# Moving small operations and a normalization to GpSimd, and reordering logits and diffusions, in the second top-p attention of a graph network

## The chip, the cores and the metric

The kernel runs on one core of a Trainium2 chip. The metric is the device time of one execution in microseconds; the figure for the kernel is the median of three runs. One further execution was recorded by the profiler. Engines are called PE (matrix products), DVE (VectorE), ACT (ScalarE), POOL (GpSimd) and SP (which issues DMAs).

## The reference

Four graph layers follow each other, each with a residual and a layer normalization, on x of 3327 x 256 and a dense adjacency matrix of 3327 x 3327, all in float32: a mean aggregation, a Mamba block, an attention over the edges, and a diffusion with top-p attention. The change concerns the last:

```
def _top_p_attention(X, W1, W2, W3):
    q = X @ W1.T @ W2.T
    k = X @ W3.T
    probs = softmax(q @ k.T)
    # sorted by size, an entry is kept while the sum of those before it is under 0.9
    A = probs * mask
    return A / maximum(A.sum(-1, keepdims=True), 1e-12)

R = (S + I) / row sums
Xf = Xa = X;  Z = 0
for n in range(2):
    A = _top_p_attention(Xa, W1, W2, W3)
    Xf = R @ Xf
    Xa = A @ Xa
    Z = Z + Xf @ U1[n].T + Xa @ U2[n].T
h = X + Z
out = (h - mean(h)) / sqrt(var(h) + 1e-5) * ln_g + ln_b
# and the layer's residual: x = layernorm(x + out)
```

## The kernel before

Rows are padded to 3328 and handled as 26 tiles of 128 rows. A tile's scores are one buffer `e` of 128 x 3328 in SBUF; each half of it has 1664 columns. The last layer has two attentions, p = 0 and p = 1, each with its own loop over the tiles. The change is in the loop of the second. In it Xf of the first step has already been multiplied by U1 (the array `Y`, stored in `F`), Xa by U2 (`G`), and what both give the result of the first step, plus the residual, lies in DRAM as `sd`, so that for a tile the second attention computes

- `diffused`: R @ Y for 128 rows, 26 products on PE whose left sides `at` come by DMA, 5 blocks at a time (`aggregated`); POOL prepares t = Y * rdeg (L823) and adds s, loaded from sd (L827); DVE writes xf (L832). `xfs` collects these tiles ahead of their use, `DL` says how far.
- `scores`: the logits, four pairs of products of 416 columns on PE (L797) into one PSUM buffer `sc`, which ACT copies to e (L782 through a helper that pins the order).
- `search_long`: finds the value v at which the kept sum passes 0.9 of the total, without sorting. ACT makes a first exponential with half the exponent for a guess (L926), then e itself with its total (L928). A threshold c1 is guessed from the two sums (L932 to L934); ACT counts and sums what lies above c1 (L940, L942); a chain of operations of 128 x 1 on DVE gives a better threshold c2 (L944 to L960); ACT counts again (L973, L975); a second chain gives c3 (L977 to L986). DVE then writes z, the entries below c3, for each half (L992), takes the 8 largest of each segment of 128 (MAX8, L858), ranks them (`ranked`, L869 and L871), runs a prefix sum over the 48 largest (`crossing`, L878 to L881), and so finds v. Ties at v are counted (L1004 to L1014), surplus ones removed by MATCH_REPLACE (L1017), and everything below v is set to zero with the kept sum as by-product (L1025).
- `attended`: A @ G: 26 transposes of e on PE (L842), copies `wt` on ACT, 26 products (L846).
- `second`: h = acc * f + xf on DVE (L1069), its statistics (`stats`, bn_stats L84 and bn_aggr L85), the inverse deviation rs by a power on POOL (L593, L594), h = (h - mean) * g (L1077), h = h * rs + xb (L1078) on DVE, where POOL has made xb = X + b (L1071); then a second normalization, with nb = -mean * rs on POOL (L1085) and the write of the result by ACT (L1086) and a DMA.

The loop is a software pipeline written by hand. In turn i, tile i is searched, tile i - 1 is attended, tile i + 2's logits are made, a tile is diffused and tile i - 2's result written. All of these are Python generators, and each `next` emits one step; `slot` emits some products of the diffusion, a step of `attended` and a step of a search. The order on each engine comes from a scheduler that works on this program; `keep_in_program_order` (also called `here`) fixes an operation's place among those so marked, `high_priority` lets operations go ahead of others that are ready, and `issue_after` ties the MATCH_REPLACE to the step that gives c2. The loop begins at i = -2.

Of the kernel before, what the change touches and what calls it, by code (L numbers as in the profile page):

```python
# [9 lines left out]
F32 = mybir.dt.float32  # L10
# [8 lines left out]
P = 128  # L19
# [18 lines left out]
J3 = 5  # L38
DL = 2
KC = 416  # L40
# [3 lines left out]
def gnn_kernel(ctx: ExitStack, tc: tile.TileContext, n: int, a: dict, out: bass.AP):  # L44
# [36 lines left out]

    def stats(mv, y):
        st = small.tile([P, 6], F32, name="bnst")
        nc.vector.bn_stats(st, y)  # L84
        nc.vector.bn_aggr(mv, st)  # L85
# [498 lines left out]
    with tc.tile_pool(name="l3", bufs=1) as pool, tc.tile_pool(name="l3d", bufs=1, space=DRAM) as dram:  # L584
# [178 lines left out]
        u1, u2 = (load(pool, x) for x in ("U1", "U2"))  # L763
        g3, b3 = (load_row(pool, x) for x in ("ln3_g", "ln3_b"))
        ones = pool.tile([P, 8 * max(RP0, RPT)], F32, name="ones")
        nc.vector.memset(ones, 1.0)
# [12 lines left out]
        tots, vs, kepts = ([pool.tile([P, nt], F32, name=f"{x}{p}") for p in range(2)] for x in ("tot", "v", "kept"))  # L779

        def in_order(op):
            return lambda *x, **k: tc.keep_in_program_order(op(*x, **k))  # L782

        def scores(work, psum, p, q, e):

            copy = in_order(nc.scalar.copy) if p else nc.scalar.copy
            if npad > n:
                nc.gpsimd.memset(e[:, n:], NEG)
            halves = e.rearrange("p (h c) -> p h c", h=2)
            for c0 in range(0, half, KC):  # L790
                pl = psum.tile([P, 2, 512], F32, name="sc", bufs=1)
                ws = [min(KC, n - c0 - h * half) for h in range(2)]

                with tc.high_priority():
                    for h, w in enumerate(ws):
                        k = slice(h * DA, (h + 1) * DA)
                        nc.tensor.matmul(pl[:, h, :w], q[k, :], kT[p][k, c0:c0 + w], start=True, stop=True)  # L797
# [75 lines left out]

        def crossing(work, v, top, base, lim):

            k = top.shape[1]
            cs = work.tile([P, k], F32, name="cs", bufs=1)
            nc.vector.tensor_tensor_scan(cs, ones[:, :k], top, initial=base, op0=ALU.mult, op1=ALU.add)  # L878
            over = work.tile([P, k], F32, name="over", bufs=1)
            nc.vector.scalar_tensor_tensor(over, cs, lim, top, op0=ALU.is_ge, op1=ALU.mult)  # L880
            nc.vector.reduce_max(v, over, axis=AX.X)  # L881
            return cs
# [22 lines left out]

        here = tc.keep_in_program_order
        junks = [None]
        bound = [None]

        def search_long(work, sm, e, total, v, kept, halves=False):  # L910
# [7 lines left out]

            m8, neg, hneg, root = t1(sm, "m8", 8), t("neg"), t("hneg"), t("root")
            nc.vector.max(m8, e[:, :KC])  # L920
            nc.vector.tensor_scalar_mul(hneg, m8[:, 0:1], -0.5)
            nc.vector.tensor_scalar_mul(neg, m8[:, 0:1], -1.0)

            junk = junks[0] = junks[0] or work.tile([P, npad], BF16, name="junk", bufs=1)
            yield
            here(nc.scalar.activation(junk, e, AF.Exp, bias=hneg, scale=0.5, accum_out=root))  # L926
            yield
            here(nc.scalar.activation(e, e, AF.Exp, bias=neg, accum_out=total))  # L928
            yield
            lim = limit(sm, total)  # L930
            c1 = t("c1")
# [15 lines left out]
            nc.vector.reciprocal(rc, c1)  # L947
            nc.vector.tensor_scalar(na, m1, lim, rc, op0=ALU.subtract, op1=ALU.mult)

# [12 lines left out]
            big = t("big")  # L962
            nc.vector.tensor_sub(big, k1, na)
            nc.vector.tensor_scalar(big, big, 32.0, HUGE, op0=ALU.is_lt, op1=ALU.mult)

            s, dm, lo, hi = t("s"), t("dm"), t("lo"), t("hi")
            nc.vector.tensor_sub(s, c2, c1)
            nc.vector.scalar_tensor_tensor(s, s, 0.0, s, op0=ALU.is_equal, op1=ALU.add)
            nc.vector.reciprocal(s, s)
            nc.vector.tensor_scalar(lo, k1, 0.3, 1.0, op0=ALU.mult, op1=ALU.max)  # L970
            nc.vector.tensor_scalar(hi, k1, 1.5, 1.0, op0=ALU.mult, op1=ALU.max)
            yield
# [4 lines left out]
            nc.vector.tensor_scalar(k2, sg, -0.5, npad / 2, op0=ALU.mult, op1=ALU.add)  # L977
            nc.vector.scalar_tensor_tensor(m2, k2, c2, f2, op0=ALU.mult, op1=ALU.add)
            nc.vector.tensor_sub(dm, m1, m2)
            nc.vector.tensor_mul(s, s, dm)  # L980
            nc.vector.tensor_scalar(s, s, lo, hi, op0=ALU.max, op1=ALU.min)
            nc.vector.reciprocal(s, s)
            c3 = t("c3")
            nc.vector.scalar_tensor_tensor(c3, c2, UNDER, m2, op0=ALU.mult, op1=ALU.add)
            nc.vector.tensor_scalar(c3, c3, lim, s, op0=ALU.subtract, op1=ALU.mult)
            nc.vector.scalar_tensor_tensor(c3, c3, c2, big, op0=ALU.add, op1=ALU.max)  # L986
            rest, base = t("rest"), t("base")
            cand = candidates(work)
            for h, r in enumerate((rest, base)):
                part = e[:, h * half:(h + 1) * half]  # L990
                z = work.tile([P, half], F32, name="z", bufs=1)
                nc.vector.scalar_tensor_tensor(z, part, c3, part, op0=ALU.is_lt, op1=ALU.mult, accum_out=r)  # L992
                yield
                segment_tops(cand[:, h * half // SEG * 8:], z, half // SEG)
                yield
            nc.vector.tensor_scalar(base, base, rest, total, op0=ALU.add, op1=ALU.subtract)
            nc.vector.scalar_tensor_tensor(base, big, 1.0, base, op0=ALU.is_lt, op1=ALU.mult)
            nc.vector.tensor_scalar_mul(base, base, -1.0)
            top = ranked(work, cand, RPT)
            cs = crossing(work, v, top, base, lim)  # L1000
            yield

            r, up = t("r"), t("up")
            nc.vector.tensor_sub(cs, cs, top)  # L1004
            nc.vector.tensor_scalar(top, top, v, None, op0=ALU.is_equal)
            nc.vector.scalar_tensor_tensor(cs, cs, lim, top, op0=ALU.is_ge, op1=ALU.mult, accum_out=r)
            upper = cand[:, half // SEG * 8:]
            nc.vector.tensor_scalar(upper, upper, v, 0.0, op0=ALU.is_equal, op1=ALU.add, accum_out=up)
            nc.vector.tensor_sub(up, r, up)
            sums = t1(sm, "sums", 2)  # L1010
            for i, (r, c) in enumerate(((up, 0), (r, half))):
                drop = t1(sm, "drop", 8)
                nc.vector.tensor_scalar(drop, count, r, -HUGE, op0=ALU.is_ge, op1=ALU.mult)  # L1013
                nc.vector.tensor_scalar_add(drop, drop, v)  # L1014
                part = e[:, c:c + half]
# [50 lines left out]
        def second(work, psum, it, acc, f, xf):  # L1066
# [9 lines left out]
            yield  # L1076
            nc.vector.scalar_tensor_tensor(h, h, mv[:, 0:1], g3, op0=ALU.subtract, op1=ALU.mult)  # L1077
            nc.vector.scalar_tensor_tensor(h, h, rs, xb, op0=ALU.mult, op1=ALU.add)  # L1078
            mv = small.tile([P, 2], F32, name="mv")
            stats(mv, h)  # L1080
            rs = small.tile([P, 1], F32, name="rs")
# [37 lines left out]
        with tc.tile_pool(name="l3w", bufs=2) as work, tc.tile_pool(name="l3s", bufs=4) as sm, \  # L1119
# [41 lines left out]
            with tc.tile_pool(name="l3q", bufs=3, space=PSUM) as psum:  # L1161
                es, searches, xfs = {}, {}, []
                result = iter(())
                for i in range(-2, nt + 1):
# [7 lines left out]
                    if i + 2 < nt:  # L1172
                        logits = start(1, i + 2, es, searches, search_long)
                    more = range(len(xfs), min(nt, max(i, 0) + DL + 1))
                    if more:
                        spread = diffused(work, atp, psum, 1, more[0], xfs, 1)

                    def slot(products, looks, pair=False):


                        if pair:
                            next(logits, None)
                        for _ in range(products):
                            next(spread, None)
                        next(values, None)
                        search(looks)
# [7 lines left out]
                    next(logits, None)  # L1194
                    next(result, None)
                    search(i + 2)
                    for _ in range(3):
                        next(spread, None)
                    next(values, None)
                    search(i)  # L1200
                    for _ in result:
                        pass
                    slot(3, i + 1, True)
                    slot(3, i + 1, True)
                    both(logits)
# [157 lines left out]
```

## Time and profile before

| | before |
|---|---|
| median of 3 runs | 3810.78 us (3806.26 to 3815.26) |
| the profiled execution | 3813.28 us, of it the span 3811.5 us |
| first attention | 1994 to 2911 us, PE busy over 99% |
| second attention | 2911 to 3811 us |
| busy: PE, DVE, ACT, POOL | 3482.6, 2626.2, 1739.7, 497.9 us |
| granted clock of PE, mean | 0.961 |

Busy times are sums over the span and differ much by stage. A row of the timeline has the start in the span, the duration, the engine, the line of the kernel, the operation and its output and inputs, then shapes; in brackets the idle time before it and what ended it. A row of the waits has who waited for whom, the sum in microseconds, how often, and the longest.

### The profile page before, as it was taken

What the parts mean: (1) busy time and instruction counts of PE and PEld (TensorE: products, weight loads), DVE (VectorE), ACT (ScalarE), POOL (GpSimd) and SP (SyncE); (2) the same over time, 40 slices, a digit from 0 to 9 for tenths busy, and PEclk for the clock granted to TensorE, in tenths of its full rate; (3) what the DMA queues carried; (4) which work ended last, traced back from release to release, by engine and by line L of the source; (5) the groups of instructions that cost most, each with busy time, mean ns of one, the idle gap of its engine ahead of it and who ended that gap; (6) DMA issues with size and microseconds to landing.
All of it is one profiled execution on the core that took longest, in us unless ns stands there. A gap on an engine that the chain in (4) does not pass through costs nothing. (4 is left out here: it accounts for less than half of the span.)

```text
span 3811.5 us, 42006 instructions
## 1 busy us (share of the span) xinstructions
PE 3482.6 (91%) x15079; PEld 2570.3 (67%) x15079; DVE 2626.2 (69%) x5640; ACT 1739.7 (46%) x2612; POOL 497.9 (13%) x760
## 2 busy tenths in 40 slices
PE   8999999888989778689999999999999899999995
PEld 7888876554545334368877777777777676666764
DVE  1111588898989899957755444444442999999996
ACT  0000655554545465311113333333335878877773
POOL 0000122222212222111110000000000111111111
PEclk9999999998989888889999999999999999999997
DMA  7442221110111000034422221122112222222210
GB/s 230 144 136 96 78 64 50 43 42 31 42 36 43 12 0 0 0 133 141 149 90 74 63 60 52 55 63 60 53 55 61 64 65 61 63 63 61 63 51 7
DMA packets 115508, 252.99 MB, mean 66 GB/s; under 512 B 16450, under 2 KB 57410, under 8 KB 115154
## 3 DMA queue, kind: packets, MB, share of 16 engines
q1 hardware_dynamic: 115282, 250.14, 21.5%
q8 instruction: 122, 2.00, 0.2%
q14 instruction: 104, 0.85, 0.1%
HBM read 239.86 MB, written 10.22 MB: 66 GB/s over the span
## 5 line engine op out<-in xcount | busy, mean ns | idle before, releaser
L473 DVE TENSOR_TENSOR_SCAN h<-dA,db 128x2052 f32<-128x2052 f32 (+3 forms) x128 | 463.8, 3624 | 6.0 <-PE y L557 3.5
L460 ACT ACTIVATE dA<-dt,A_log 128x512 f32<-128x512 f32 (+3 forms) x512 | 296.3, 635 | 331.6 <-DVE h L473 277.8
L557 PE MATMUL y<-h,ident 128*128 128x512 f32 (+3 forms) x1024 | 436.9, 564 | 3.2 <-DVE h L549 3.2
L557 PEld LDWEIGHTS y<-h,ident 128*128 128x128 f32 x1024 | 200.7, 208 | 251.3 <-issue 225.6
L846 PE MATMUL acc<-G,wt 128*128 128x256 f32 x1352 | 345.7, 397 | 11.7 <-ACT wt L782 11.2
L846 PE MATMUL acc<-X,wt 128*128 128x256 f32 x1352 | 343.6, 391 | 8.3 <-ACT wt L844 8.0
L813 PE MATMUL acc<-F,at 128*128 128x256 f32 x1352 | 339.3, 380 | 1.7 <-ACT q L604 0.6
L846 PEld LDWEIGHTS acc<-G,wt 128*128 128x128 f32 x1352 | 247.2, 193 | 112.3 <-ACT wt L782 46.2
L116 PE MATMUL acc<-xa,at 128*128 128x257 f32 x1352 | 309.9, 383 | 5.8 <-DMA at<-in_adjT 5.7
L813 PE MATMUL acc<-X,at 128*128 128x256 f32 x1352 | 309.5, 382 | 3.0 <-issue 2.8
L846 PEld LDWEIGHTS acc<-X,wt 128*128 128x128 f32 x1352 | 242.5, 189 | 103.2 <-issue 41.3
L732 PE MATMUL acc<-F,at 128*128 128x257 f32 x1352 | 307.3, 384 | 4.9 <-DVE at L729 4.9
L264 PE MATMUL cb<-F,at 128*128 128x256 f32 x1352 | 309.6, 381 | 1.6 <-ACT hn L283 1.6
L466 DVE TENSOR_TENSOR db<-du,row 128x2048 f32<-128x2048 f32 (+3 forms) x128 | 240.0, 1878 | 84.3 <-ACT row L448 84.1
L858 DVE MAX8 cand<-e 128x8 f32<-128x128 f32 x676 | 142.1, 278 | 226.2 <-ACT e L799 214.6
L264 PEld LDWEIGHTS cb<-F,at 128*128 128x128 f32 x1352 | 256.5, 191 | 58.6 <-issue 17.6
L116 PEld LDWEIGHTS acc<-xa,at 128*128 128x128 f32 x1352 | 256.5, 191 | 43.3 <-issue 6.2
L732 PEld LDWEIGHTS acc<-F,at 128*128 128x128 f32 x1352 | 255.9, 192 | 41.6 <-issue 5.2
L813 PEld LDWEIGHTS acc<-X,at 128*128 128x128 f32 x1352 | 253.7, 191 | 43.2 <-issue 10.2
L813 PEld LDWEIGHTS acc<-F,at 128*128 128x128 f32 x1352 | 243.2, 190 | 39.2 <-issue 7.8
L549 DVE TENSOR_TENSOR h<-h,C 128x2048 f32<-128x2048 f32 (+3 forms) x128 | 240.8, 1881 | 38.2 <-PE C L484 25.2
L797 PE MATMUL sc<-kT,q 64*128 64x416 f32 x832 | 201.5, 561 | 37.7 <-ACT e L782 34.3
(308 smaller groups left out, 5320.0 us busy)
## 6 DMA issues: line engine op xcount, KB each, us to landing
at<-in_adjT SPq DMA_DIRECT2D x102, 832.0 KB, 4.5
at<-in_adjT SPq DMA_DIRECT2D x260, 320.0 KB, 3.0
at<-in_adjT SPq DMA_DIRECT2D x52, 576.0 KB, 3.7
at<-in_adjT SPq DMA_DIRECT2D x26, 512.0 KB, 3.6
xt<-in_xT SPq DMA_DIRECT2D x26, 128.0 KB, 4.1
qd<-q SPq DMA_DIRECT2D x104, 32.0 KB, 1.9
q<-qd SPq DMA_DIRECT2D x52, 64.0 KB, 1.9
at<-in_adjT SPq DMA_DIRECT2D x52, 64.0 KB, 1.8
```

Source lines behind the costliest of these rows:

```text
L116: nc.tensor.matmul(acc, at[:, j, :], rhs[:, j0 + j, :], start=(j0 + j == 0), stop=(j0 + j == nt - 1))
L264: nc.tensor.matmul(acc, at[:, j % JC, :], X0[:, j, :], start=(j == 0), stop=(j == nt - 1))
L460: nc.scalar.activation(dA[:, g, 1:], dt[:, g, :], AF.Exp, scale=A[:, g, s:s + 1])
L466: nc.vector.tensor_mul(by_group(dbs[s % 2], w)[:, :, 1:], du, B.to_broadcast([P, NG, w]))
L473: nc.vector.tensor_tensor_scan(h[:, :m], dAs[s % 2][:, :m], dbs[s % 2][:, :m], initial=0.0, op0=ALU.mult, op1=ALU.add)
L549: nc.vector.tensor_mul(h, h, C.to_broadcast([P, NG, w]))
L557: nc.tensor.matmul(ys[g][:, :w], ident, h[:, g, :], start=False, stop=(s == DS - 1))
L732: nc.tensor.matmul(acc, at[:, j, :], F[:, j0 + j, :], start=(j0 + j == 0), stop=(j0 + j == nt - 1))
L797: nc.tensor.matmul(pl[:, h, :w], q[k, :], kT[p][k, c0:c0 + w], start=True, stop=True)
L813: nc.tensor.matmul(acc, at[:, j, :], rhs[:, j0 + j, :], start=(j0 + j == 0), stop=(j0 + j == nt - 1))
L846: nc.tensor.matmul(acc, wt[:, j, :], rhs[:, j0 + j, :], start=(j0 + j == 0), stop=(j0 + j == nt - 1))
L858: nc.vector.max(cand[:, s * 8:(s + 1) * 8], z[:, s * SEG:(s + 1) * SEG])
```

## The change

In the second attention: POOL makes the two scaled maxima that the exponentials need, the limit, the reciprocal's input s, its two bounds `ends` and `big`, and the base of the prefix sum, partly as one operation of two columns; the limit and the base have their signs turned, so that `crossing` subtracts and compares the other way. The two drops of ties are made by one pair of operations instead of two. The normalization of the result by mean, deviation, g and xb is three operations on POOL, followed by a step of its own ahead of the second statistics, whose bn_stats is pinned in order. The logits' products of this attention are pinned in program order without priority, and their copies are steps of their own. DL is 3 instead of 2, and the first diffusions are spread over the turns i = -2, -1 and 0 instead of following each other at the end of the first. The second half's z is pinned too.

```diff
-DL = 2
+DL = 3
...
-    def stats(mv, y):
+    def stats(mv, y, order=lambda x: x):
         st = small.tile([P, 6], F32, name="bnst")
-        nc.vector.bn_stats(st, y)
+        order(nc.vector.bn_stats(st, y))
         nc.vector.bn_aggr(mv, st)
...
+        factors = pool.tile([P, 4], F32, name="factors")
+        for k, x in enumerate((-0.5, -1.0, 0.3, 1.5)):
+            nc.vector.memset(factors[:, k:k + 1], x)
...  scores
-                with tc.high_priority():
+                with tc.high_priority() if not p else nullcontext():
                     for h, w in enumerate(ws):
                         k = slice(h * DA, (h + 1) * DA)
-                        nc.tensor.matmul(pl[:, h, :w], q[k, :], kT[p][k, c0:c0 + w], start=True, stop=True)
+                        mm = nc.tensor.matmul(pl[:, h, :w], q[k, :], kT[p][k, c0:c0 + w], start=True, stop=True)
+                        if p:
+                            here(mm)
+                if p:
+                    yield
...  search_long
-            nc.vector.tensor_scalar_mul(hneg, m8[:, 0:1], -0.5)
-            nc.vector.tensor_scalar_mul(neg, m8[:, 0:1], -1.0)
+            nc.gpsimd.tensor_scalar(neg, factors[:, :2], m8[:, 0:1], None, op0=ALU.mult)
...
-            lim = limit(sm, total)
+            lim = t("lim")
+            nc.gpsimd.tensor_scalar(lim, total, -TOP_P, None, op0=ALU.mult)
...
-            nc.vector.tensor_sub(big, k1, na)
-            nc.vector.tensor_scalar(big, big, 32.0, HUGE, op0=ALU.is_lt, op1=ALU.mult)
-
-            s, dm, lo, hi = t("s"), t("dm"), t("lo"), t("hi")
-            nc.vector.tensor_sub(s, c2, c1)
-            nc.vector.scalar_tensor_tensor(s, s, 0.0, s, op0=ALU.is_equal, op1=ALU.add)
-            nc.vector.reciprocal(s, s)
-            nc.vector.tensor_scalar(lo, k1, 0.3, 1.0, op0=ALU.mult, op1=ALU.max)
-            nc.vector.tensor_scalar(hi, k1, 1.5, 1.0, op0=ALU.mult, op1=ALU.max)
+            nc.gpsimd.tensor_tensor(big, k1, na, op=ALU.subtract)
+            nc.gpsimd.tensor_scalar(big, big, 32.0, HUGE, op0=ALU.is_lt, op1=ALU.mult)
+
+            s, dm, ends, same = t("s"), t("dm"), t1(sm, "ends", 2), t("same")
+            nc.gpsimd.tensor_tensor(s, c2, c1, op=ALU.subtract)
+            nc.gpsimd.tensor_scalar(same, s, 0.0, None, op0=ALU.is_equal)
+            nc.gpsimd.tensor_tensor(s, s, same, op=ALU.add)
+            nc.gpsimd.tensor_scalar(ends, factors[:, 2:], k1, 1.0, op0=ALU.mult, op1=ALU.max)
...
+            nc.vector.reciprocal(s, s)
             nc.vector.tensor_sub(dm, m1, m2)
             nc.vector.tensor_mul(s, s, dm)
-            nc.vector.tensor_scalar(s, s, lo, hi, op0=ALU.max, op1=ALU.min)
+            nc.vector.tensor_scalar(s, s, ends[:, 0:1], ends[:, 1:2], op0=ALU.max, op1=ALU.min)
...
-                nc.vector.scalar_tensor_tensor(z, part, c3, part, op0=ALU.is_lt, op1=ALU.mult, accum_out=r)
+                x = nc.vector.scalar_tensor_tensor(z, part, c3, part, op0=ALU.is_lt, op1=ALU.mult, accum_out=r)
+                if h:
+                    here(x)
...
-            nc.vector.tensor_scalar(base, base, rest, total, op0=ALU.add, op1=ALU.subtract)
-            nc.vector.scalar_tensor_tensor(base, big, 1.0, base, op0=ALU.is_lt, op1=ALU.mult)
-            nc.vector.tensor_scalar_mul(base, base, -1.0)
+            nc.gpsimd.tensor_scalar(base, base, rest, total, op0=ALU.add, op1=ALU.subtract)
+            nc.gpsimd.tensor_scalar(rest, big, 1.0, base, op0=ALU.is_lt, op1=ALU.mult)
+            base = rest
...
-            for i, (r, c) in enumerate(((up, 0), (r, half))):
-                drop = t1(sm, "drop", 8)
-                nc.vector.tensor_scalar(drop, count, r, -HUGE, op0=ALU.is_ge, op1=ALU.mult)
-                nc.vector.tensor_scalar_add(drop, drop, v)
+            drops = sm.tile([P, 2, 8], F32, name="drop")
+            nc.vector.tensor_tensor(drops, count[:, None, :].to_broadcast([P, 2, 8]),
+                                    r[:, :, None].to_broadcast([P, 2, 8]), op=ALU.is_ge)
+            nc.vector.tensor_scalar(drops, drops, -HUGE, v, op0=ALU.mult, op1=ALU.add)
...  second
-            nc.vector.scalar_tensor_tensor(h, h, mv[:, 0:1], g3, op0=ALU.subtract, op1=ALU.mult)
-            nc.vector.scalar_tensor_tensor(h, h, rs, xb, op0=ALU.mult, op1=ALU.add)
+            nc.gpsimd.tensor_scalar(h, h, mv[:, 0:1], rs, op0=ALU.subtract, op1=ALU.mult)
+            nc.gpsimd.tensor_tensor(h, h, g3, op=ALU.mult)
+            nc.gpsimd.tensor_tensor(h, h, xb, op=ALU.add)
+            yield
             mv = small.tile([P, 2], F32, name="mv")
-            stats(mv, h)
+            stats(mv, h, here)
...  the loop of the second attention
-                    more = range(len(xfs), min(nt, max(i, 0) + DL + 1))
-                    if more:
-                        spread = diffused(work, atp, psum, 1, more[0], xfs, 1)
+                    more = range(len(xfs), min(nt, i + DL + 1))
+                    spread = (x for j in more for x in diffused(work, atp, psum, 1, j, xfs, 1))
...  slot
                         if pair:
                             next(logits, None)
-                        for _ in range(products):
+                        for _ in range(products * len(more)):
                             next(spread, None)
+                        if pair:
+                            next(logits, None)
...
                     next(logits, None)
                     next(result, None)
+                    for _ in range(3 * len(more)):
+                        next(spread, None)
+                    next(logits, None)
                     search(i + 2)
-                    for _ in range(3):
-                        next(spread, None)
                     next(values, None)
                     search(i)
+                    next(result, None)
+                    slot(3, i + 1, True)
+                    slot(3, i + 1, True)
                     for _ in result:
                         pass
-                    slot(3, i + 1, True)
-                    slot(3, i + 1, True)
                     both(logits)
...
-                    for j in more[1:]:
-                        both(diffused(work, atp, psum, 1, j, xfs))
```

More of the change, by code (lines that the diff above doesn't have):

```diff
@@ L1 @@
 import math
-from contextlib import ExitStack
+from contextlib import ExitStack, nullcontext
 import concourse.bass as bass
@@ L779, in gnn_kernel @@
         tots, vs, kepts = ([pool.tile([P, nt], F32, name=f"{x}{p}") for p in range(2)] for x in ("tot", "v", "kept"))
+        here = tc.keep_in_program_order
         def in_order(op):
@@ L872, in ranked, with crossing @@
             return top
-        def crossing(work, v, top, base, lim):
+        def crossing(work, v, top, base, lim, add=ALU.add, reached=ALU.is_ge):
             k = top.shape[1]
             cs = work.tile([P, k], F32, name="cs", bufs=1)
-            nc.vector.tensor_tensor_scan(cs, ones[:, :k], top, initial=base, op0=ALU.mult, op1=ALU.add)
+            nc.vector.tensor_tensor_scan(cs, ones[:, :k], top, initial=base, op0=ALU.mult, op1=add)
             over = work.tile([P, k], F32, name="over", bufs=1)
-            nc.vector.scalar_tensor_tensor(over, cs, lim, top, op0=ALU.is_ge, op1=ALU.mult)
+            nc.vector.scalar_tensor_tensor(over, cs, lim, top, op0=reached, op1=ALU.mult)
             nc.vector.reduce_max(v, over, axis=AX.X)
@@ L904, in search_short @@
             yield
-        here = tc.keep_in_program_order
         junks = [None]
@@ L917, in t @@
                 return t1(sm, name)
-            m8, neg, hneg, root = t1(sm, "m8", 8), t("neg"), t("hneg"), t("root")
+            m8, neg, root = t1(sm, "m8", 8), t1(sm, "neg", 2), t("root")
             nc.vector.max(m8, e[:, :KC])
-            nc.vector.tensor_scalar_mul(hneg, m8[:, 0:1], -0.5)
-            nc.vector.tensor_scalar_mul(neg, m8[:, 0:1], -1.0)
+            nc.gpsimd.tensor_scalar(neg, factors[:, :2], m8[:, 0:1], None, op0=ALU.mult)
             junk = junks[0] = junks[0] or work.tile([P, npad], BF16, name="junk", bufs=1)
             yield
-            here(nc.scalar.activation(junk, e, AF.Exp, bias=hneg, scale=0.5, accum_out=root))
+            here(nc.scalar.activation(junk, e, AF.Exp, bias=neg[:, 0:1], scale=0.5, accum_out=root))
             yield
-            here(nc.scalar.activation(e, e, AF.Exp, bias=neg, accum_out=total))
+            here(nc.scalar.activation(e, e, AF.Exp, bias=neg[:, 1:2], accum_out=total))
             yield
-            lim = limit(sm, total)
+            lim = t("lim")
+            nc.gpsimd.tensor_scalar(lim, total, -TOP_P, None, op0=ALU.mult)
             c1 = t("c1")
@@ L947, in search_long @@
             nc.vector.reciprocal(rc, c1)
-            nc.vector.tensor_scalar(na, m1, lim, rc, op0=ALU.subtract, op1=ALU.mult)
+            nc.vector.tensor_scalar(na, m1, lim, rc, op0=ALU.add, op1=ALU.mult)
             den, nu, p, q = t("den"), t("nu"), t("p"), t("q")
@@ L984, in search_long @@
             nc.vector.scalar_tensor_tensor(c3, c2, UNDER, m2, op0=ALU.mult, op1=ALU.add)
-            nc.vector.tensor_scalar(c3, c3, lim, s, op0=ALU.subtract, op1=ALU.mult)
+            nc.vector.tensor_scalar(c3, c3, lim, s, op0=ALU.add, op1=ALU.mult)
             nc.vector.scalar_tensor_tensor(c3, c3, c2, big, op0=ALU.add, op1=ALU.max)
@@ L995, in search_long @@
                 yield
-            nc.vector.tensor_scalar(base, base, rest, total, op0=ALU.add, op1=ALU.subtract)
-            nc.vector.scalar_tensor_tensor(base, big, 1.0, base, op0=ALU.is_lt, op1=ALU.mult)
-            nc.vector.tensor_scalar_mul(base, base, -1.0)
+            nc.gpsimd.tensor_scalar(base, base, rest, total, op0=ALU.add, op1=ALU.subtract)
+            nc.gpsimd.tensor_scalar(rest, big, 1.0, base, op0=ALU.is_lt, op1=ALU.mult)
+            base = rest
             top = ranked(work, cand, RPT)
-            cs = crossing(work, v, top, base, lim)
+            cs = crossing(work, v, top, base, lim, ALU.subtract, ALU.is_le)
             yield
-            r, up = t("r"), t("up")
-            nc.vector.tensor_sub(cs, cs, top)
+            r = t1(sm, "r", 2)
+            nc.vector.tensor_add(cs, cs, top)
             nc.vector.tensor_scalar(top, top, v, None, op0=ALU.is_equal)
-            nc.vector.scalar_tensor_tensor(cs, cs, lim, top, op0=ALU.is_ge, op1=ALU.mult, accum_out=r)
+            nc.vector.scalar_tensor_tensor(cs, cs, lim, top, op0=ALU.is_le, op1=ALU.mult, accum_out=r[:, 1:])
             upper = cand[:, half // SEG * 8:]
-            nc.vector.tensor_scalar(upper, upper, v, 0.0, op0=ALU.is_equal, op1=ALU.add, accum_out=up)
-            nc.vector.tensor_sub(up, r, up)
+            nc.vector.tensor_scalar(upper, upper, v, 0.0, op0=ALU.is_equal, op1=ALU.add, accum_out=r[:, :1])
+            nc.vector.tensor_sub(r[:, :1], r[:, 1:], r[:, :1])
+            drops = sm.tile([P, 2, 8], F32, name="drop")
+            nc.vector.tensor_tensor(drops, count[:, None, :].to_broadcast([P, 2, 8]),
+                                    r[:, :, None].to_broadcast([P, 2, 8]), op=ALU.is_ge)
+            nc.vector.tensor_scalar(drops, drops, -HUGE, v, op0=ALU.mult, op1=ALU.add)
             sums = t1(sm, "sums", 2)
-            for i, (r, c) in enumerate(((up, 0), (r, half))):
-                drop = t1(sm, "drop", 8)
-                nc.vector.tensor_scalar(drop, count, r, -HUGE, op0=ALU.is_ge, op1=ALU.mult)
-                nc.vector.tensor_scalar_add(drop, drop, v)
+            for i, c in enumerate((0, half)):
+                drop = drops[:, i, :]
                 part = e[:, c:c + half]
```

## The prediction

> **What bounds the kernel now.** I read the page first, then the starts of the large mask z (L992), one per tile, in the second attention; then its waits and its timeline.
>
> ```profile
> PE 3482.6 (91%) x15079; PEld 2570.3 (67%) x15079; DVE 2626.2 (69%) x5640; ACT 1739.7 (46%) x2612; POOL 497.9 (13%) x760
> DVE 20%; PE 1%; issue 1%; POOL 1%; ACT 1%; ACTq 0%; POOLq 0%; DVEq 0%
> 3200.00:3300.00 100.00, 92.44 (x448) 70.04 (x447) 94.87 (x354) 79.34 (x79) 15.47 (x31) 1.00 0.22 62
> ```
>
> Over the whole span PE is busiest, but the chain that ended last is DVE for 20% of the span, and these are the last 760 us. The third line is 100 us of the second attention: columns PE, PEld, DVE, ACT, POOL busy, clock, DMA. DVE is at 95. The first z of a tile starts at 2951.31, 2979.23, 3009.48, 3038.98, 3071.41, then 18 times every 32.77 us, and the last intervals are 32.52, 32.14 and 28.88: 803.5 us for 25 intervals, then 56.7 us of tail. So a microsecond taken off one tile's DVE loop is worth some 22 us. What the others wait for (14 tiles, 3202 to 3660):
>
> ```profile
> ACT junk L940 <- DVE nc L938: 22.6, 14, 1.9
> PE sc L797 <- ACT e L782: 19.7, 14, 1.7
> PE tp L842 <- DVE e L1025: 15.6, 14, 1.1
> DVE h L1078 <- POOL rs L594: 10.7, 14, 0.8
> ```
>
> ACT idles 1.6 us a tile on DVE, PE 1.41 on ACT and 1.11 on DVE, while DVE's own only wait is 0.77. PE's work in a tile is therefore at most 32.77 - 2.5 = 30.3: the next bound, 2.5 below DVE.
>
> **DVE's loop, by stretches.** The place with most to win is the one behind the first statistics:
>
> ```profile
> 3230.28 0.18 DVE L85 BATCH_NORM_AGGREGATE mv<-bnst 128x2 f32<-128x6 f32 x1
> 3230.50 0.49 DVE L1077 SCALAR_TENSOR_TENSOR h<-h,mv,ln_g 128x256 f32<-128x256 f32 x1
> 3231.75 0.49 DVE L1078 SCALAR_TENSOR_TENSOR h<-h,rs,t 128x256 f32<-128x256 f32 x1 [0.77 <-POOL rs L594]
> 3232.16 0.15 DVE L977 TENSOR_SCALAR k<-sg 128x1 f32<-128x1 f32 x1
> 3233.51 0.63 DVE L980 TENSOR_TENSOR s<-s,dm 128x1 f32<-128x1 f32 x1
> 3235.25 1.95 DVE L992 SCALAR_TENSOR_TENSOR z<-e,c 128x1664 f32<-128x1664 f32 x1
> ```
>
> From L85 to z it is 4.97 us. L980 takes 0.63 for one element a partition; alone it takes 0.125. I rebuilt the changed queue from these rows, starting a dependent operation 0.04 us after the end of its producer, an independent one 0.08 before the end of the one ahead:
> - z to first MAX8 over the candidates: 9.35 before, 9.85 after. The chain for c1 (0.19 a step) now stands whole between the first 13 MAX8 and the second z (+0.32), the second bn_stats stands here (0.35), lim and one base go (-0.24; the rest is rounding).
> - candidates to scan: 4.82 and 4.82; the other two base operations sat in latencies.
> - scan to k1: 2.46, 2.30 (one drop pair less). k1 to the first MATCH_REPLACE: 2.04, 1.97; lo, hi and big also filled latencies of the c2 chain, so removing them returns almost nothing.
> - to the mask of e (L1025): 3.92, 3.85. To L85: 5.22, 5.35.
> - L85 to z: 4.97, 2.34. L1077, its wait and L1078 go (1.66), L980's stall (0.50), the small neg and hneg, and the second statistics.
>
> Sum: 32.78 to 30.48, if GpSimd disturbs nothing.
>
> **What GpSimd costs DVE.** Its rows around that stall:
>
> ```profile
> 3232.34 0.96 POOL L823 TENSOR_SCALAR t<-F,rdeg 128x256 f32<-128x256 f32 x1 [0.62 <-DVE k L977]
> 3233.38 0.74 POOL L827 TENSOR_TENSOR t<-t,s 128x256 f32<-128x256 f32 x1
> 3234.10 0.22 POOL L593 TENSOR_SCALAR rs<-mv 128x1 f32<-128x1 f32 x1
> 3234.40 0.57 POOL L594 TENSOR_TENSOR rs<-rs,mhalf 128x1 f32<-128x1 f32 x1
> ```
>
> L980 ends when POOL's two-input L827 ends: two operations with two SBUF inputs exclude each other. It holds the other way too: L827 took up to 2.08 us and L594 2.12 when they met a z. A z that began 0.59 us into L823, with one input, was not delayed, and the MAX8, bn_stats and MATCH_REPLACE rows show no stretching.
> The Trainium skill, GPSIMD Engine Reference, section Specifications, states this contention for DVE instructions with two SBUF inputs; section Key points adds that DVE is structurally about twice as fast for elementwise work, which speaks against this change, and agrees in kind with 0.73 against 0.48 here. By the factor alone, 0.97 us of two DVE steps becomes 1.9 on GpSimd; the rows below give 2.7, and I go by them.
>
> GpSimd gets three large operations a tile: h by mean and rs (the same form, L751 of layer 2, 1.23 us; with one scalar L823 is 0.95), times g (0.73, as L1071), plus xb (0.73). After L85 come L593 and L594 (1.0), so it reaches the product with g 0.1 to 0.4 us before z is due. Either DVE's z waits for it, up to 0.73, or it waits for z and then, with the sum and the two diffusion operations (0.95, 0.73), meets the c1 chain and the second z 4.7 us later. I charge 0.6, near L980's stall of 0.50. The bounds are 0, and 2.9 when all four two-input 128x256 operations of a tile each hold DVE for their 0.73. That gives **31.1 us a tile** (30.5 to 33.4). The ten small operations (0.2 to 0.28 each, about 2.4 us) lie beside z's MAX8s and the MATCH_REPLACEs, where DVE has one input. The second bn_stats, pinned behind z's second MAX8s at 9.5 us, leaves GpSimd 10 us for h: no wait (with one, the ranking MAX8s behind it, and through them the whole loop, would stand). The neg for ACT and the load of s on SP stand behind the sum with s; both are needed some 8 us later. ACT's write of the result moves behind L942, and c1 arrives 1.6 us earlier in the tile after the 1.6 us wait shown above, so ACT stays under 30; behind that write stand only wt's copies, for which ACT itself waits on PE (58.0 us in 42 waits of the same window).
>
> Intervals at 31.1: 21 that took 686.95 become 653.1 (-33.9); the last -1.5; the first, without a normalization, -0.3; the second and third, 30.25 and 29.50 before without a diffusion, now hold one: +2. Together -33.7.
>
> **The start.** In the second attention's first turn, ACT now:
>
> ```profile
> 2922.77 3.07 ACT L926 ACTIVATE junk<-e,hneg 128x3328 bf16<-128x3328 f32 x1
> 2925.84 0.83 ACT L782 COPY e<-sc 128x832 f32<-128x832 f32 x1
> 2926.57 3.07 ACT L928 ACTIVATE e<-e,neg 128x3328 f32<-128x3328 f32 x1
> ```
>
> The copy is of tile 1's first logits, which the priority lifted between tile 0's diffusion products. In the changed order PE has 18 products and tile 0's four pairs first, then 34 more products (two spread diffusions), then tile 1's first pair; and ACT has tile 1's copy pinned ahead of the second exponential of tile 0. By PE's rows (32 halves of products in 7.19 us, so 0.45 a product; a pair 0.9): 2911.2 + 18 x 0.45 + 4 x 0.9 = 2922.9, + 34 x 0.45 + 0.9 = 2939.1, + 0.85 for the copy = 2940: the exponential starts 13.4 later, and the first z, behind the same ACT steps, some **13 later**. DVE, the bound from then on, doesn't win it back. Bounds: 0, if tile 1's logits came early after all, and 13.4.
>
> **The tail.** The last tile's normalization lies open: for 0.52 of L1078 (start to next start) now 1.23 + 0.73 + 0.73 and three gaps of 0.04 = 2.8, so +2.3; less 0.6 for small steps that the last searches lose. +1.7. The first attention is bound by PE, its work is the same (the extra diffusion is only taken from its end): 0, within 1. The four memsets lie under earlier work: 0, 0.3 if not.
>
> **Sum.** -33.7 + 13 + 1.7 = -19. The profiled execution, 3813.28 (span 3811.5 and 1.8 around it), becomes 3794.3; it lay 2.5 above the median of the runs, 3810.78, so **3792** there. One us a tile is 22.5 us in the total.
>
> **Rivals.**
> 1. Contention eats the gain (slower). One mechanism: GpSimd's two-input products of the normalization hold DVE's two-input steps in the c3 chain, z and the c1 chain. Break-even is at 31.95 us a tile (19/22.5 above my figure), that is 1.45 us of held DVE instead of 0.6. At 2.2 us (three of the four large ones in full) 32.7 a tile: -33.7 + 36 + 14.7, so +17, 3828. For it: 0.50 lost to a single L827; nothing in before shows three in a row. Against: most of DVE's steps in that stretch have one input, and GpSimd waits too.
> 2. Better than said: contention near 0 (30.5 a tile, -13.5 more: 3778), or the start not delayed (3779). For it: POOL may find z already running, and then waits itself. Below 30.3 PE holds it.
> 3. PE's waits don't shrink: with logits in program order PE stands behind ACT's copies of sc (one buffer, 1.41 a tile now). 30.3 + 1.4 = 31.7 a tile: +13.5, 3805. Against: these waits exist because ACT is itself held by DVE.
> 4. The normalization isn't hidden because bn_stats waits: needs GpSimd 10 us late; the rows sum to under 6. It has no share of its own.
>
> **Chances.** 0.2%, 7.6 us, is about what a measurement of this kernel can tell from no change. Forecast (30.9 to 31.5 a tile, 3787 to 3801) 0.45 and rival 2 (from 3765, both of its parts, to 3787) 0.20: faster. Rival 3 (3801 to 3812) 0.12: no change. Rival 1 (from 3812) 0.23: 0.05 of it no change, 0.18 slower. So faster 0.65, same 0.17, slower 0.18. The range of 8 in 10 leaves out the low end of rival 2 (0.05) and the upper part of rival 1 (0.15): 3773 to 3820.
>
> **What would show it.** Right: z starts 31.1 us apart; no DVE wait on rs; the product of s and dm (L980) near 0.13 us, or a z starting late beside a POOL product; the first z at 2964; PE's waits on ACT and DVE down to about 0.8 a tile; 2.3 us more between the last h and its write. Wrong: first z at 2951 (no start loss), intervals of 32 or more with DVE's small operations stretched, or DVE with idle time before bn_stats on POOL h.

## The result and the profile after

The changed kernel takes 3790.14 us (median of 4 runs, 3785.42 to 3797.4) against 3808.52 us of the kernel before (also the median of 4): a ratio of 0.9952, 95% interval 0.9929 to 0.9975, so some 18 us less (10 to 27). In a second comparison, below, the ratio was 0.996 (0.9948 to 0.9972). The forecast was 3792 and 19 us less. The interval is wide, so 18 beside 19 is closer than the parts of the forecast deserve: in the traces, below, the second attention alone gained 22.5 us.

The page of the changed kernel, and 100 us of its second attention (columns: PE, PEld, DVE, ACT, POOL busy, clock, DMA share, GB/s):

```profile
PE 3482.1 (92%) x15079; PEld 2564.3 (68%) x15079; DVE 2591.0 (68%) x5228; ACT 1739.9 (46%) x2612; POOL 668.0 (18%) x1098
3300.00:3400.00 100.00, 98.37 (x472) 72.66 (x470) 96.03 (x325) 81.80 (x79) 38.09 (x74) 1.00 0.23 69
```

DVE has lost 35 us of work and 412 instructions, POOL gained 170 us. PE now stands at 98% in this stage, DVE at 96%, which reads as if PE were the bound. It isn't yet, as experiment e7 shows. Of the waits between 3202 and 3640 us one is of PE and none of DVE. These are the last two rows of the list:

```profile
PE tp L852 <- DVE e L1039: 8.2, 15, 0.6
POOL big L972 <- DVE den L961: 2.6, 14, 0.2
```

DVE waits for nobody here; PE's wait for the mask of e has fallen from 1.1 us a tile to 0.55, and its wait for ACT's copies of the logits is gone from the list.

The profiled execution took 3788.17 us, its span 3786.4. The spans of before and after differ by 25.1 us, but 2.5 of these lie before 1994 us, in layers whose instructions are the same: over all runs of this study the first diffusion product of the second attention comes between 2904.7 and 2912.8 us. I therefore count the second attention from that product: 900.3 us before, 877.7 after, 22.5 us less. It is made up of

| from the trace, us | before | after | forecast | measured |
|---|---|---|---|---|
| first diffusion product to the first z | 40.1 | 54.3 | +13 | +14.2 |
| first z to last z, 25 intervals | 803.5 | 765.9 | -33.7 | -37.6 |
| one interval in the middle | 32.77 | 30.95 | 31.1 | 30.95 |
| last z to the end | 56.7 | 57.6 | +1.7 | +0.9 |

One stretch of DVE's timeline in the changed kernel answers to the one shown of before:

```profile
3327.07 0.18 DVE L85 BATCH_NORM_AGGREGATE mv<-bnst 128x2 f32<-128x6 f32 x1
3327.17 0.12 DVE L985 TENSOR_SCALAR k<-sg 128x1 f32<-128x1 f32 x1
3327.77 0.16 DVE L989 TENSOR_TENSOR s<-s,dm 128x1 f32<-128x1 f32 x1
3328.16 0.58 DVE L929 MAX8 m<-e 128x8 f32<-128x416 f32 x1
3329.40 1.95 DVE L1001 SCALAR_TENSOR_TENSOR z<-e,c 128x1664 f32<-128x1664 f32 x1
```

From the aggregation of the first statistics to z it is now 2.33 us instead of 4.97 (I had rebuilt 2.34): the two normalizing steps and their wait are gone, and the product of s and dm (L989, L980 before) takes 0.16 instead of 0.63. The loss to GpSimd has moved to another place. One tile earlier, first POOL's lines, then DVE's:

```profile
3298.74 2.24 POOL L1092 TENSOR_TENSOR h<-h,ln_g 128x256 f32<-128x256 f32 x1
3301.06 0.72 POOL L1093 TENSOR_TENSOR h<-h,t 128x256 f32<-128x256 f32 x1
3302.92 0.73 POOL L837 TENSOR_TENSOR t<-t,s 128x256 f32<-128x256 f32 x1
```

```profile
3298.45 1.95 DVE L1001 SCALAR_TENSOR_TENSOR z<-e,c 128x1664 f32<-128x1664 f32 x1
3302.97 0.70 DVE L942 TENSOR_TENSOR c<-c,tot 128x1 f32<-128x1 f32 x1
```

z is 0.3 us ahead of POOL's product with g, which then needs 2.24 us instead of 0.72: it ends 0.58 us behind z, as if it had stood until z was over. This pushes POOL's queue back, until its sum t + s begins 0.05 us ahead of DVE's first step for c1; that step, on one element a partition, needs 0.70 us and ends with the sum. In these rows the loser is the one that came second.

### The profile page after: what moved, and what is told of

The parts are those of the page before. It is cut to its first block, busy times and chain, and to the rows that moved or that the text cites. A ratio compares the mean times of both kernels' runs of the same rounds, so it can differ in the third digit from the quotient of the medians.

```text
span 3786.4 us, 41877 instructions
## 1 busy us (share of the span) xinstructions
PE 3482.1 (92%) x15079; PEld 2564.3 (68%) x15079; DVE 2591.0 (68%) x5228; ACT 1739.9 (46%) x2612; POOL 668.0 (18%) x1098
## 4 chain that ended last, share of the span: by engine, by line
PE 48%; DVE 37%; issue 6%; ACT 4%; POOL 4%; DMA 1%; SPq 0%; POOLq 0%; DVEq 0%; ACTq 0%
DVE h L473 9%; PE acc L856 9%; PE acc L823 8%; PE acc L116 7%; PE acc L732 7%; DVE cand L868 4%; DVE h L549 3%; PE sc L803 3%; DVE z L1001 3%; DVE e L1031 2%; DVE db L466 2%; PE y L557 2%; PE cb L264 2%; DVE e L1039 2%; PE tp L852 2%
## 5 line engine op out<-in xcount | busy, mean ns | idle before, releaser
L856 PE MATMUL acc<-G,wt 128*128 128x256 f32 x1352 | 337.8, 393 | 18.2 <-ACT wt L787 17.8
L823 PE MATMUL acc<-F,at 128*128 128x256 f32 x1352 | 347.8, 385 | 1.0 <-ACT q L604 0.6
L476 POOL COPY carry<-h 128x4 f32<-128x4 f32 x128 | 117.1, 915 | 846.0 <-DVE h L473 831.0
```

The source lines that it names most:

```text
L476: nc.gpsimd.tensor_copy(carry[:, s, :], h[:, :, w])
L823: nc.tensor.matmul(acc, at[:, j, :], rhs[:, j0 + j, :], start=(j0 + j == 0), stop=(j0 + j == nt - 1))
L856: nc.tensor.matmul(acc, wt[:, j, :], rhs[:, j0 + j, :], start=(j0 + j == 0), stop=(j0 + j == nt - 1))
```

## The experiments

Totals below are single executions unless a ratio is given. The middle interval (z to z) is the better measure, since within a trace it mostly repeats to 0.05 us (30.91 to 30.96 in the changed kernel).

**e1, the normalization back on DVE.**

```diff
-            nc.gpsimd.tensor_scalar(h, h, mv[:, 0:1], rs, op0=ALU.subtract, op1=ALU.mult)
-            nc.gpsimd.tensor_tensor(h, h, g3, op=ALU.mult)
-            nc.gpsimd.tensor_tensor(h, h, xb, op=ALU.add)
+            nc.vector.scalar_tensor_tensor(h, h, mv[:, 0:1], g3, op0=ALU.subtract, op1=ALU.mult)
+            nc.vector.scalar_tensor_tensor(h, h, rs, xb, op0=ALU.mult, op1=ALU.add)
```

> The two operations of the result's normalization are back on DVE, all else as changed. By the theory that DVE's queue bounds a tile, start-to-start time of the rows is added: 1.25 us for the first with its wait on rs, 0.41 for the second, less 0 to 0.5 if GpSimd's sum with s no longer meets the first step of c1 (0.70 us instead of 0.20 in the changed kernel): 32.1 to 32.6 us a tile instead of 30.95. By the rival that PE (98% busy in the changed kernel) bounds it, 31.0 to 31.3.

Measured: 32.17 us a tile, 3817.48 us in all. The wait is back at its old length, and the stall at c1 is gone:

```profile
3406.70 0.48 DVE L1092 SCALAR_TENSOR_TENSOR h<-h,rs,t 128x256 f32<-128x256 f32 x1 [0.77 <-POOL rs L594]
...
3411.42 0.15 DVE L942 TENSOR_TENSOR c<-c,tot 128x1 f32<-128x1 f32 x1
```

The normalization on GpSimd is worth 1.22 us a tile, net of what it costs at c1. Without it the rest of the change gains nothing: from the first diffusion product to the end it is 904.8 us, against 900.3 before, of which the later start is 14.0 (the totals of single runs, 3817.48 against 3809.61, differ by no more than executions of one kernel do).

**e2, the ten small operations back on DVE.** In `search_long` every `nc.gpsimd.` becomes `nc.vector.`:

```diff
-            nc.gpsimd.tensor_tensor(big, k1, na, op=ALU.subtract)
+            nc.vector.tensor_tensor(big, k1, na, op=ALU.subtract)
...
```

> The ten small operations of the search are back on DVE, in their new form, the normalization stays on GpSimd. By the rebuilt queue, most of them fill latencies of chains: 0.3 to 0.6 us more a tile, 31.2 to 31.5. By the rival that each costs its own duration of some 0.15 us: 32.4. By the rival that PE bounds the tile: 30.95.

Measured: 31.42 us a tile, 3800.91 us in all. The small operations are worth 0.47 us a tile, about a third of the 1.5 us that ten operations of some 0.15 us would add: most of them lay in latencies of chains. With e1, 1.69 of the 1.82 us that a tile gained are accounted for; the 0.13 left would be the merged drops and the new order, if the parts add up, which no run here shows.

**e3, without t + s.**

```diff
             if p:
-                s = work.tile([P, D], F32, name="s")
-                nc.sync.dma_start(s, sd[it])
-                nc.gpsimd.tensor_tensor(t, t, s, op=ALU.add)
+                pass
```

> Left out: the load of s and its addition to t on GpSimd, so the result lacks the first step's part. GpSimd's last two-input operation ahead of the c1 chain is gone. By the contention theory the first step of c1 takes 0.20 us instead of 0.70, and a tile 30.4 to 30.5 us instead of 30.95. By the rival that PE bounds the tile, 30.9.

Measured: 3777.36 us in all; in the middle of the loop tiles of 30.37 us, and later a cycle of 30.37, 30.48, 30.59 and 30.93 (mean 30.6). The step at c1:

```profile
3419.39 0.14 DVE L940 TENSOR_TENSOR c<-c,tot 128x1 f32<-128x1 f32 x1
```

(In this kernel the line is 940.) 0.70 became 0.14, so the collision at this place costs 0.56 us, and the tiles of 30.37 lie 0.11 under the rebuilt 30.48 without collisions. In the longest tiles z itself is stretched, from 1.95 to 2.51 us, because POOL's product with g (L1090 here) now meets z at its very beginning:

```profile
3353.58 2.51 DVE L999 SCALAR_TENSOR_TENSOR z<-e,c 128x1664 f32<-128x1664 f32 x1
```

```profile
3353.61 0.73 POOL L1090 TENSOR_TENSOR h<-h,ln_g 128x256 f32<-128x256 f32 x1
```

This is the other of the prediction's two ways, DVE's z waiting for POOL, and it costs the same 0.56 us. In the tile before, where POOL's product began 0.05 us behind z instead of 0.03, POOL lost (2.49 us). So the tiles of 30.93 are no sign that PE is the bound. PE is at 99.4% now (298.11 of 300 us) and may be what shifts the order slowly from tile to tile; no run tests that.

**e4, one buffer for t, one for xb.** The two had shared two buffers.

```diff
-            t = work.tile([P, D], F32, name="t")
+            t = work.tile([P, D], F32, name="t", bufs=1)
...
-            xb = work.tile([P, D], F32, name="t")
+            xb = work.tile([P, D], F32, name="xb", bufs=1)
```

> t gets one buffer and xb one of its own, instead of two that they share. In the order that results GpSimd makes t and its sum with s directly behind xf, beside bn_stats, and xb behind the normalization, some 0.3 us ahead of the c1 chain. Same result. By the contention theory the stall of 0.5 us at c1 goes: 30.4 to 30.6 us a tile. By the rival that PE bounds it, 30.9; and if GpSimd's sum meets a step of DVE behind xf, the stall only moves: 30.9 too, but with a stretched DVE operation between xf and z.

Measured: 30.62 us a tile, 3782.26 us in all. The step at c1 takes 0.14 us again, and a part of the loss has moved to the step that t + s now meets (L837 is POOL's, L986 DVE's; 0.22 in the changed kernel):

```profile
3386.40 0.72 POOL L837 TENSOR_TENSOR t<-t,s 128x256 f32<-128x256 f32 x1
```

```profile
3386.67 0.47 DVE L986 SCALAR_TENSOR_TENSOR m<-k,c,fs 128x1 f32<-128x1 f32 x1
3393.52 0.14 DVE L942 TENSOR_TENSOR c<-c,tot 128x1 f32<-128x1 f32 x1
```

-0.56 + 0.25 = -0.31, against -0.33 measured between the intervals; 30.62 is at the upper end of the expected 30.4 to 30.6. Moving GpSimd's sum, without taking it away, moves the price.

**e5 and e6, fewer diffusions in the first turn.** In the second attention's loop (the comments only tell the two runs apart):

```diff
-                    more = range(len(xfs), min(nt, i + DL + 1))
+                    more = range(len(xfs), min(nt, i + 3))      # e5
+                    more = range(len(xfs), min(nt, i + 2))      # e6
```

> One diffusion instead of two in the second attention's first turn, and so one turn less ahead for all later ones. By my reading of the start, PE has 9 products fewer ahead of tile 0's last logits and 17 instead of 34 between them and tile 1's first: at 0.45 us each 4 + 7.7 = 11.7 us earlier for the second exponential, so the first z 42.6 us behind the first diffusion product instead of 54.3, tiles of 30.95 us, and 11 to 12 us off the total. By the rival that the start is set by ACT's own steps, the first z stays at 54.

> No diffusion in the second attention's first turn, one in each later one. The order then has tile 1's first logits 3 products behind tile 0's last, as in the kernel before. By my reading the first z comes 40 us behind the first diffusion product (before: 40.1; changed: 54.3), and the total is 14 us shorter than the changed kernel's, with tiles of 30.95 us. If the diffusions were needed earlier than this, a wait of DVE for PE of some microseconds appears in the first tiles, and the gain is smaller by it.

Measured: the first z 42.3 us (e5) and 40.05 us (e6) behind the first diffusion product, tiles 30.96 us in both; 3774.73 and 3768.73 us in all. The exponential whose delay the prediction priced, in the changed kernel and in e6:

```profile
2937.49 0.85 ACT L787 COPY e<-sc 128x832 f32<-128x832 f32 x1 [12.40 <-PE sc L803]
2938.24 3.07 ACT L936 ACTIVATE e<-e,neg 128x3328 f32<-128x3328 f32 x1
```

```profile
2920.10 3.07 ACT L936 ACTIVATE e<-e,neg 128x3328 f32<-128x3328 f32 x1
```

In the first, ACT stands 12.4 us for tile 1's first logits, which are behind 34 products on PE. Counted from the first diffusion product (2908.6 and 2904.7) the exponential comes at 29.6 and 15.4 us. In e5 and e6 the changed kernel's one long interval near the end (32.41, in which DVE waits 1.89 us for PE's last product) is also 30.97: perhaps because the diffusions there end later; I didn't test it. From e6's 862.2 us (first product to the end) to the changed kernel's 877.7 it is 15.5.

**e7, 20 of 26 products.** Left out: the last 6 products of each diffusion of the second attention.

```diff
-                    nc.tensor.matmul(acc, at[:, j, :], rhs[:, j0 + j, :],
-                                     start=(j0 + j == 0), stop=(j0 + j == nt - 1))
+                    last = min(19, nt - 1) if each == 1 else nt - 1
+                    if j0 + j <= last:
+                        nc.tensor.matmul(acc, at[:, j, :], rhs[:, j0 + j, :],
+                                         start=(j0 + j == 0), stop=(j0 + j == last))
```

> Left out: the last 6 of the 26 products of each diffusion of the second attention, so PE has 2.7 us less in each tile. If DVE bounds a tile, it stays at 30.95 us and PE idles 3 us of it; the first z comes some 4 us earlier (9 products fewer ahead of tile 1's logits). If PE, 98% busy, is what bounds the changed kernel, tiles take 28.3 to 29 us.

Measured: 30.96 us a tile, the first z at 49.85 us, 3780.53 us in all.

```profile
3300.00:3600.00 300.00, 273.22 (x1300) 205.39 (x1298) 288.44 (x957) 249.61 (x245) 121.89 (x213) 0.98 0.23 68
```

PE falls to 91% and the tile stays where it was. So in the changed kernel DVE is the bound, though PE shows the higher share.

**e8, the logits' priority restored.**

```diff
-                with tc.high_priority() if not p else nullcontext():
+                with tc.high_priority():
...
-                        if p:
-                            here(mm)
```

> The logits' products have their priority back and no pinned place; the copies stay steps of their own, two diffusions in the first turn. The order has tile 1's first logits 3 products behind tile 0's last again. By my reading the first z comes 40 us behind the first diffusion product, as before, and tiles stay at 30.95 us, since DVE bounds them: 14 us shorter than the changed kernel. By the rival that the pinned logits are what keeps PE's waits short, tiles take 31.5 us and the gain is lost again.

Measured: the first z 40.05 us behind the first product, tiles of 31.06 us, 865.6 us from first product to end (changed: 877.7), 3780.23 us in all. The pinned logits cost the late start only together with diffusions in the first turn (14.2 us with two, 2.2 with one in e5); either remedy brings the 14 us back. In the steady state pinning them gains 0.1 us a tile.

**e10, the second statistics without their place.**

```diff
             nc.gpsimd.tensor_tensor(h, h, xb, op=ALU.add)
-            yield
...
-            stats(mv, h, here)
+            stats(mv, h)
```

> The normalization on GpSimd is not a step of its own, and the second bn_stats has no pinned place: the order has it ahead of z, some 0.7 us behind the first statistics, instead of behind the second MAX8s. By my reading GpSimd has h ready 3.9 us behind the first statistics (1.0 for rs, 2.7 and gaps), so DVE waits 3.2 us there, less the 0.5 of the stall at c1: 33.6 to 34.2 us a tile, slower than the kernel before (32.77). By the rival that it is only the order of cheap operations, 31 us and no wait.

Measured: 33.72 us a tile, 3855.28 us in all.

```profile
3424.77 0.43 DVE L84 BATCH_NORM_STATS2 bnst<-h 128x6 f32<-128x256 f32 x1 [3.34 <-POOL h L1093]
```

This is the rival that had no share of its own: DVE waiting for the normalization. The profile of the changed kernel can't show it, because the step of its own and the pinned place keep it away. This run takes both away together; they are worth 2.8 us a tile, more than the whole gain. Against e1, where DVE normalizes (32.17), a normalization on GpSimd with its consumer at once loses 1.55 us a tile.

**e9, e4 and e6 together, and the changed kernel beside it.**

> No diffusion in the first turn (as in the run before that did it alone) and one buffer for t with one for xb (as in that run): the two gains together, same result. They sit in different places, so they add: 14 us from the start and 0.33 us a tile over some 20 tiles, 6.5 us, so about 20 us under the changed kernel, 3765 to 3772, a ratio to the kernel before near 0.990. By the rival that PE (99% busy in tiles of 30.6) now bounds the loop and the later diffusions cost it, the second gain is gone: ratio 0.992.

> The changed kernel once more, beside the version with both alterations: tiles of 30.95 us, a ratio to the kernel before of 0.994 to 0.996.

Measured: 3761.9 us, ratio to before 0.9879 (0.9864 to 0.9893); the changed kernel 3792.25 us, ratio 0.996 (0.9948 to 0.9972). In the traces the first z comes at 40.05 us instead of 54.1, tiles take 30.62 instead of 30.96, and from the first diffusion product to the end it is 854.8 instead of 878.3 us: 23.5 less, a little more than the 20 expected. The medians differ by 30, and 3761.9 lies 3 us under the expected range; the two profiled executions differ by 23.8, so I put the rest down to the scatter of executions (3786.67 to 3800.2 for the changed kernel). This version beats both kernels.

## Why the prediction was right, step by step

- **The bound and the rebuilt queue.** Right. DVE bounds the changed kernel (e7); for the kernel before it rests on the waits in its profile, where DVE had one of 0.77 us a tile. Its queue without collisions was put at 30.48; e3, without the sum that collides at c1, runs at 30.37 where no other collision comes.
- **The price of GpSimd.** Right in mechanism, place and, nearly, size: 0.6 charged; 30.95 - 30.48 = 0.47 by my queue and 0.56 by the stretched step. Of the two ways offered, the second came: POOL waits for z and then meets the c1 chain. It was near: POOL reached its product with g 0.3 us behind z, not 0.1 to 0.4 ahead of it as reckoned; had it come first, e3's long tiles show about the same price, 0.56.
- **What excludes what.** Too narrow in the prediction, which has two operations with two inputs exclude each other. A one-input operation of GpSimd was held as well, when DVE's had two inputs. It happened in the kernel before, in the rows behind the first statistics:

```profile
3230.56 0.51 POOL L593 TENSOR_SCALAR rs<-mv 128x1 f32<-128x1 f32 x1 [0.41 <-DVE mv L85]
```

  Alone L593 takes 0.22 us; here it began 0.06 us behind DVE's L1077, and so 0.29 of the 0.77 us that DVE then waits for rs are a collision that DVE made itself. In the other direction the prediction's reading holds: in the changed kernel z began in 24 tiles beside POOL's one-input step L1091 and was never delayed by more than 0.03 us. The Trainium skill, GPSIMD Engine Reference, section Specifications, says that the two engines contend when DVE has two SBUF inputs. The rows stretched here (L593 by L1077, L1092 by z, L942 and L986 by L837) all have such a DVE operation.
- **The slower engine.** The Trainium skill, GPSIMD Engine Reference, section Key points, has DVE about twice as fast for elementwise work. Here a two-input 128x256 operation took 0.73 us on GpSimd and 0.48 on DVE. A slower engine was no argument against this change: three operations of 2.7 us on GpSimd replaced 1.66 us of DVE's queue at a net gain of 1.22, because the wait of e10 was designed away.
- **The small operations.** Right: worth 0.47 a tile by e2; the rebuilt queue says the same, that most of them sit in latencies.
- **The intervals' sum.** -33.7 forecast, -37.6 measured. The 16 middle intervals at 30.95 instead of 31.1 make 2.4 of the difference, the three ahead of them (31.20, 30.55, 30.63) 0.9 and the two behind them 0.5. The second and third interval grew by 0.8 instead of 2, and the first and the last together fell by 0.8 instead of 1.8: these two misses nearly cancel.
- **The start.** Right: 13 forecast, 14.2 measured, a little over the forecast's own upper bound of 13.4. The trace has the 18 and the 34 products as counted, but the two stretches took 12.2 and 15.7 us instead of 11.7 and 15.3. e5, e6 and e8 took the cause away in part or whole and returned 12.0, 14.2 and 14.2 us.
- **The tail.** Forecast +1.7, measured +0.9. The exposed normalization itself was as priced: from rs to the second bn_stats 3.0 us instead of 0.55. What remains as relief elsewhere in the tail is 1.5 instead of my 0.6; I did not trace it further.
- **The first attention.** No change: from its first diffusion product to that of the second attention 916.6 us before and after, though in the other runs this stretch lay between 916.5 and 921.0. PE is busy for 902 of these 917 us before, 98.4%, and over 99% only from 2100 to 2800 us.
- **The rivals.** The slower one had a break-even of 31.95 a tile; nothing came near it. The third (PE's waits stay) is excluded by e7 and by the waits that shrank. The second didn't come: both of its parts were real possibilities, as e9 shows, but not of this change.

## What to carry to other kernels

An engine at 98% busy need not be the bound: take some of its work away and see whether the period moves (here it stayed at 30.96 us). When work is handed to a second engine, the gain depends on where the consumer stands in the first engine's queue: against the same work on DVE 1.2 us a tile were gained with the consumer some ten microseconds later, and 1.55 lost with it at once. And a change to a steady loop should be counted at its ends too: here the first turn gave back 14 of 38 us, by an order that one changed line (e6) undoes.

## What the runs showed of the hardware

- An operation of DVE with two inputs in SBUF and a two-input one of GpSimd on 128x256 hold each other off, in both directions: DVE's 128x1 step L942 took 0.70 us instead of 0.14 when a 128x256 sum had begun 0.05 us before it, and GpSimd's 128x256 product 2.24 instead of 0.72 behind a z of 1.95 us.
- With one input on GpSimd's side it goes almost only one way. GpSimd's one-input operations stood behind DVE's two-input ones: L593 took 0.51 instead of 0.22 us before, and in e4 L833 took 4.31 instead of 0.95 behind the mask of e (3.68). DVE's z was not delayed by L1091 in the changed kernel (24 tiles, 0.03 us at most); the most that I found one of DVE's two-input operations stretched beside a one-input one was 0.25 us, in e3.
- h = acc * f + xf (L1083), which reads acc from PSUM, was not stretched in 17 tiles in which it began beside the two-input L1085 with some 0.6 us of that left.
- The time up to the second attention lay between 2904.7 and 2912.8 us in the runs of this study. I have no cause for it; it is as large as the 0.2% that the prediction takes for what can be told from no change. A steady interval, which mostly repeats to 0.05 us, is the better measure. Counting a stage from its own first instruction helps less: the second attention of the changed kernel took 877.7 and 878.3 us in its two traces, but the first still varied by 4.5.
